# Four graph attention layers on one core: layer 3's neighbour terms by a plain transfer, masked maxima on VectorE, a changed scheduler and shared small tiles

## The chip, the cores and the metric

The kernel runs on one core of a Trainium2 chip. TensorE (PE) multiplies matrices and transposes, VectorE (DVE), ScalarE (ACT) and GpSimd (POOL) work on tiles of 128 partitions, SyncE (SP) issues DMA transfers, and so can POOL, whose transfers can add to what lies at their destination. The metric is the device time of one execution in microseconds; less is better. All data are float32, but for the int32 adjacency matrices.

## The reference, cut to what matters

There are 128 graphs of 128 nodes with 512 features (`x`), and one adjacency matrix each (`adj`). Four attention layers follow each other, each on a normalised copy of x, with a residual sum:

```python
h = jnp.maximum(_layernorm(x, axis=-1), 0.0)
x = x + _L0_gnn_ref(h, adj, W, a1, a2)              # one head, elu
h = jnp.maximum(_layernorm(x, axis=-1), 0.0)
x = x + _L1_gnn_ref(adj, h, ...)                    # 4 heads of 256, elu, then 1 head of 512
h = jnp.maximum(_layernorm(x, axis=-1), 0.0)
x = x + _L2_gnn_ref(h, adj, w_src, w_dst, b)        # one head on h itself
h = jnp.maximum(_layernorm(x, axis=-1), 0.0)
x = x + _L3_gnn_ref(h, adj, W_proj, W_att, b_att)   # 8 heads of 64
```

Layer 3, which the change is about:

```python
xh = (x @ W_proj).reshape(B, N, H, k).transpose(0, 2, 1, 3)
a_src = jnp.einsum('bhnk,hk->bhn', xh, W_att[:, :k])
a_dst = jnp.einsum('bhnk,hk->bhn', xh, W_att[:, k:])
scores = leaky_relu(a_src[:, :, :, None] + a_dst[:, :, None, :] + b_att[None, :, None, None], 0.2)
att = softmax(where((A > 0)[:, None], scores, -1e30), axis=-1)
out = relu(einsum('bhij,bhjk->bhik', att, xh))
```

## The kernel before

One graph is one generator, `graph(b)`: masks from the adjacency matrix, then `layer0`, `layer1`, `layer2`, `layer3`, then the store of x. Each `yield` hands one step (an instruction, or a `Group` of some that stay together) to the scheduler, or asks for a tile, a fork or a join. `FLYING` = 11 graphs are in the works at a time. The `Scheduler` runs while the program is built: with a hand-made table of durations (`Step.estimate`) it keeps a time at which each engine is free and each tile is written (`start`), and `issue` always emits the step that could start first, ties going to the lower `rank` (the graph's number and how far along it is). So the whole order of every engine is fixed at build time, and on the chip each engine runs its own list in order. Every instruction is emitted by one line, L256, so the profile has nearly everything on that line, and groups are told apart by tiles and shapes. Tiles of a tag come from a fixed number of buffers; `give_back` frees one.

Each layer begins with `norm_relu`: bn_stats and bn_aggr on DVE, + eps and the power -1/2 on POOL (tile `st`), nmr = -mean * rstd on DVE, then the relu with scale and bias on ACT into `h`. Layers 1 and 3 transpose `h` by four PE transposes into a PSUM bank, which ACT copies to `ht`, and project it (`projected`, weights `w1x`, `wpx`; layer 1's second part uses `w2x`). The scores of one-headed layers, and of layer 1, are masked and their maxima taken by `tensor_tensor_reduce` on DVE (in the profile CUSTOM_DVE_ANT_0, each with a DVE_READ_ACCUMULATOR2 behind it): add the mask, keep the maximum. In layers 0 and 2, dot products of h with a vector go the same way (`products<-h,u`).

Layer 3 holds a tile `sd` with 16 squares of 128 x 128: `d` (8 heads, rows are the nodes that receive, for the maxima) and `e` (8 heads, the other way round, for the matmuls). ACT copies the mask into d and its transpose into e, eight times each. The small matrix `f` (own and neighbour terms of 8 heads) is written to DRAM as 16 rows, and one accumulating DMA on POOL's queue (L612), broadcast to all partitions, adds them to d and e at once (1 MB). DVE reduces d to the maxima `mx`, adds the own term, ACT applies the leaky relu, DVE negates it. A second accumulating DMA (512 KB) adds the negated maxima to e after its eight Prelus; ACT takes the exponential, and PE multiplies e with `fx` head by head (128 x 65, the last column giving the sum). The last `LATE` = 5 graphs do without DRAM: `add_rows` makes the rows with PE transposes in PSUM and DVE adds them (six times 128 x 512 a graph).

Of the kernel before, what the change touches and what calls it, by code (L numbers as in the profile page):

```python
# [9 lines left out]
F32 = mybir.dt.float32  # L10
# [11 lines left out]
FLYING = 11  # L22
AHEAD = 1
# [19 lines left out]
class Step:  # L43
# [4 lines left out]
    def __init__(self, engine, method, args, kw):  # L48
# [7 lines left out]
        ins = [a for a in ins if isinstance(a, bass.AP)]  # L56
        self.writes = [a.tensor.name for a in outs]
# [3 lines left out]
    def estimate(self, name, outs, ins, kw):  # L61

        if name == "dma_start":
            moved = size(outs[0]) * outs[0].shape[0] * 4
            if self.engine == "POOL":
                self.moves = moved / 165e3
                return 1.0, 3
            run = 4 * min(a.shape[-1] for a in outs + ins)
            self.moves = moved / (280e3 if run > 512 else 220e3)
            return (0.5 if max(len(a.shape) for a in outs + ins) > 2 else 0.35), 1.5  # L70
# [68 lines left out]

class Scheduler:  # L140
    def __init__(self):
# [3 lines left out]
        self.moved = 0.0  # L145
# [86 lines left out]
    def start(self, step):  # L232
        t = self.engine_free.get(step.engine, 0.0)
        for r in step.reads:
            t = max(t, self.written.get(r, 0.0))
# [3 lines left out]
        return t  # L239

    def issue(self):
# [5 lines left out]
        if not ready:  # L247
            assert not self.streams, [vars(s.next) for s in self.streams]
            return False
        t, _, _, _, s = min(  # L250
            (self.start(s.next), self.rank(s), s.age, i, s) for i, s in enumerate(ready)
        )
        step = s.next
# [4 lines left out]
        end = t + step.busy + step.delay  # L258
        if step.moves:

            self.moved = max(end, self.moved) + step.moves
            end = self.moved + 0.3
        for name in step.writes:
            self.written[name] = end
        for name in step.reads + step.writes:
            self.last_use[name] = max(end, self.last_use.get(name, 0.0))
# [17 lines left out]
def kernel(  # L284
# [40 lines left out]
    small = ctx.enter_context(tc.tile_pool(name="small", bufs=FLYING + 2))  # L325
# [16 lines left out]

    def column(tag, n=1):
        return small.tile([P, n], F32, tag=tag, name=tag)
# [44 lines left out]
    def setup():  # L389
# [6 lines left out]
        w0 = yield tile_of("sd", 3, 2 * H3, P)  # L396
        w0 = w0.rearrange("p s q -> p (s q)").rearrange("p (c f) -> p c f", c=KC)
        for c in range(KC):
            yield S.dma_start(out=w0[:, c], in_=l0_w[c * P : (c + 1) * P])
# [25 lines left out]
        wa = yield tile_of("sd", 3, 2 * H3, P)  # L425
        wa = wa.rearrange("p s q -> p (s q)")[:, : H3 * 2 * K3]
# [5 lines left out]
    def fold_u(w0):  # L432
        us = [(yield bank()), (yield bank())]
        for c in range(KC):
            for i, u in enumerate(us):
# [3 lines left out]
                    rhs=w0[:, c, :],  # L439
# [6 lines left out]
        give_back(w0)  # L446
# [39 lines left out]
    def fold_w3(wa):  # L486
        pairs = wa.rearrange("p (h k) -> p h k", h=H3)
        for w in wpx:
            for s in range(2):
                prod = yield tile_of("t3", 2, D)  # L490
# [11 lines left out]
    def norm_relu(xt):  # L502
# [9 lines left out]
        yield V.scalar_tensor_tensor(nmr, mean, -1.0, rstd, ALU.mult, ALU.mult)  # L512
# [73 lines left out]

    def add_rows(cols, to):

        for g in range(0, cols.shape[1], 4):
            pt = yield bank()  # L590
            yield Group(
                [
                    T.transpose(
                        pt[:, j * P : (j + 1) * P],
                        cols[:, g + j : g + j + 1].to_broadcast([P, P]),
                        ident,
                    )
                    for j in range(4)
                ]
            )  # L600
# [4 lines left out]
    def added(cols, to, late, rows=None):  # L605

        if late:
            yield from add_rows(cols, to)
            return
        if rows is None:  # L610
            rows = yield from rows_in_dram(repeated(cols), cols.shape[1])
        yield G.dma_start(out=to, in_=rows, accum_op=ALU.add)  # L612

    def attention(own, rows, e, mask, exact=False):
# [4 lines left out]
        mx = column(f"mx{nh}", nh)  # L619
# [18 lines left out]
        neg = column(f"neg{nh}", nh)  # L638
        yield V.scalar_tensor_tensor(neg, mx, -1.0, own, ALU.mult, ALU.subtract)
        nm = column(f"nm{nh}", nh)  # L640
        yield V.scalar_tensor_tensor(nm, neg, SLOPE, neg, ALU.mult, ALU.min)
        z = column(f"z{nh}", nh)
# [20 lines left out]
        rz = column(f"rz{nh}", nh)  # L663
        yield V.reciprocal(rz, z)
        return rz

    def attended(own, other, mask, values, exact=False):
# [4 lines left out]
        rz = yield from attention(own, [pb[:, :P]], [e], mask, exact)  # L672
# [5 lines left out]
        return pa, rz  # L678
# [39 lines left out]
    def layer0(xt, mask):  # L718
        h = yield from norm_relu(xt)
        yield Until("u")  # L720
        f = column("f0", 2)
        yield from dot(h, u1, f[:, 0:1])
        yield from dot(h, u2, f[:, 1:2])
        t = yield tile_of("t0", 2, D)
        pa, rz = yield from attended(f[:, 0:1], f[:, 1:2], mask, h, exact=True)
        give_back(h)

        yield A.activation(out=t, in_=pa, func=AF.Exp, scale=rz)
        yield A.activation(out=pa, in_=pa, func=AF.Relu, scale=rz)
        yield V.scalar_tensor_tensor(t, t, 1.0, pa, ALU.min, ALU.add)  # L730
# [4 lines left out]
    def layer1(xt, mask, late):  # L735
# [22 lines left out]
        rz = yield from attention(fx[:, H1:E1], heads, heads, mask)  # L758
        for j in range(H1):
            yield A.activation(out=heads[j], in_=heads[j], func=AF.Copy, scale=rz[:, j : j + 1])  # L760
        if late:
# [7 lines left out]
        for g in range(0, FC, 4):  # L769
# [23 lines left out]
            t = yield tile_of("t1", 2, 4 * P)  # L793
# [11 lines left out]
        pa, rz = yield from attended(gx[:, 1:2], gx[:, 0:1], mask, gx[:, E2:])  # L805
        give_back(gx)
        yield V.scalar_tensor_tensor(xt, pa, rz, xt, ALU.mult, ALU.add)
        give_back(pa)

    def layer2(xt, mask):  # L810
        h = yield from norm_relu(xt)
        f = column("f0", 2)
        yield from dot(h, w_src, f[:, 0:1])
        yield from dot(h, w_dst, f[:, 1:2])
        fb = column("fb")
        yield G.tensor_tensor(fb, f[:, 0:1], b_l2, ALU.add)
        pa, rz = yield from attended(fb, f[:, 1:2], mask, h)
        give_back(h)
        yield V.scalar_tensor_tensor(xt, pa, rz, xt, ALU.mult, ALU.add)
        give_back(pa)  # L820

    def layer3(xt, mask, mask_t, late):
# [10 lines left out]
        sd = yield tile_of("sd", 3, 2 * H3, P)  # L833
        d, e = sd[:, :H3], sd[:, H3:]
        for to, m in (d, mask), (e, mask_t):
            yield A.copy(to, m.unsqueeze(1).to_broadcast([P, H3, P]))
            give_back(m)
# [9 lines left out]
        f = small.tile([P, 2, H3], F32, tag="f3", name="f3")  # L847
        yield G.tensor_tensor(f, fx[:, :, :E3].rearrange("p h s -> p s h"), b_l3, ALU.add)
        fork = yield Fork(
            added(f.rearrange("p s h -> p (s h)"), sd.rearrange("p s q -> p (s q)"), late)  # L850
# [161 lines left out]
```

## Time and profile before

| what | value |
|---|---|
| time, median of 3 runs | 3317.16 us (3317.16 to 3318.29) |
| the profiled execution's own time | 3315.37 us |
| its span | 3313.6 us |
| granted TensorE clock, mean | 0.992 |
| accumulating transfers (queue q0) | 193.48 MB, 31.2% of 16 engines' span |
| transfers issued by SP (queue q1) | 183.57 MB, 19.4% |

The profile is one execution on the chip. A row of a group reads: line, engine, operation, written tile <- read tiles, shapes, count, then busy us in all, mean ns of one, and the idle time of that engine just before the group with what ended it. The chain of waits is followed back from the last instruction, at each step to what released it. A row of windows gives the busy time of each engine in that stretch. Matmuls are pipelined and their ends modelled, so PE's busy share says that it always had something in hand, and the interval from start to start is the time that a matmul really costs.

### The profile page before, as it was taken

The numbers are of one execution on the slowest core, as the hardware profiler recorded it, in microseconds if no ns is written. First come the engines' busy times: TensorE is split into PE (matmuls) and PEld (weight loads), VectorE is DVE, ScalarE is ACT, GpSimd is POOL, SyncE is SP. The second block draws the span as 40 slices with busy tenths as digits, with TensorE's granted clock in tenths as the row PEclk, the third lists the DMA queues.
The fourth block names the chain that finished last, engine by engine and source line by source line (L and its number), as shares of the span: only waits on it lengthen the run. The fifth ranks groups of instructions, "written<-read, shape, count | busy, mean of one in ns | idle before, by whom it ended". The sixth has DMA issues, their size and how long they took to land.

```text
span 3313.6 us, 57764 instructions
## 1 busy us (share of the span) xinstructions
PE 3278.1 (99%) x16252; PEld 2577.0 (78%) x16252; DVE 2657.6 (80%) x9921; ACT 2600.8 (78%) x7060; POOL 954.6 (29%) x1791
## 2 busy tenths in 40 slices
PE   8999999999999999999999999999999999999997
PEld 5777777777777777777777777777777777777786
DVE  7778878878888888888888888788788878878866
ACT  5687887887888788788778878878887887887875
POOL 1123323332232332233233233323323323332221
PEclk8999999999999999999999999999999999999998
DMA  5155555455555545655555554555555555455441
GB/s 169 41 114 124 115 116 126 113 117 126 120 113 118 129 113 115 132 109 117 123 123 116 116 127 112 118 130 114 113 121 126 115 116 128 109 117 128 95 92 31
DMA packets 236001, 380.75 MB, mean 115 GB/s; under 512 B 57120, under 2 KB 136480, under 8 KB 219936
## 3 DMA queue, kind: packets, MB, share of 16 engines
q0 software_dynamic: 35424, 193.48, 31.2%
q1 hardware_dynamic: 196080, 183.57, 19.4%
q8 instruction: 129, 2.11, 0.3%
q14 instruction: 192, 1.57, 0.2%
q10 hardware_dynamic: 4176, 0.02, 0.1%
HBM read 309.35 MB, written 67.57 MB: 114 GB/s over the span
## 4 chain that ended last, share of the span: by engine, by line
PE 97%; DVE 2%; ACT 1%; issue 0%; POOL 0%; DMA 0%; POOLq 0%; ACTq 0%; DVEq 0%
PE bank L256 97%; DVE products L256 0%; DVE sd L256 0%; DVE t L256 0%; DVE st L256 0%; ACT sd L256 0%; DVE e L256 0%; DVE xt L256 0%; ACT ht L256 0%; POOL st L256 0%; DVE wpx L256 0%; DMA a<-in_L_gnn_a_dram 0%; DVE mx L256 0%; ACT h L256 0%; DVE m L256 0%
## 5 line engine op out<-in xcount | busy, mean ns | idle before, releaser
L256 PE MATMUL bank<-w2x,y 128*128 128x257 f32 x4096 | 971.8, 380 | 0.0
L256 PE MATMUL bank<-w1x,ht 128*128 128x344 f32 x3072 | 952.3, 453 | 0.0
L256 PEld LDWEIGHTS bank<-w2x,y 128*128 128x128 f32 x4096 | 740.2, 190 | 86.7 <-issue 2.6
L256 PEld LDWEIGHTS bank<-w1x,ht 128*128 128x128 f32 x3072 | 574.5, 191 | 245.9 <-issue 1.9
L256 POOL TENSOR_SCALAR st<-st 128x1 f32<-128x1 f32 x512 | 193.5, 378 | 1754.9 <-DVE st L256 1525.3
L256 PE MATMUL bank<-wpx,ht 128*128 128x264 f32 x2048 | 502.2, 389 | 1.4 <-ACT ht L256 1.4
L256 PEld LDWEIGHTS bank<-wpx,ht 128*128 128x128 f32 x2048 | 391.5, 192 | 119.2 <-issue 57.9
L256 ACT ACTIVATE h<-xt,st 128x512 f32<-128x512 f32 x512 | 415.8, 812 | 19.8 <-DVE st L256 18.2
L256 ACT COPY xl<-bank 128x344 f32<-128x344 f32 x384 | 170.9, 445 | 300.3 <-PE bank L256 300.2
L256 ACT ACTIVATE sd<-sd,f 128x128 f32<-128x128 f32 x1024 | 375.4, 393 | 0.0
L256 ACT ACTIVATE e<-e,nm 128x128 f32<-128x128 f32 x896 | 355.4, 399 | 6.8 <-DVE e L256 2.4
L256 DVE BATCH_NORM_STATS2 st<-xt 128x6 f32<-128x512 f32 x512 | 352.2, 688 | 0.0
L256 POOL TENSOR_TENSOR st<-st,minus_half 128x1 f32<-128x1 f32 x512 | 338.4, 661 | 42.4
L256 POOL DMA_DIRECT2D sd<-d x246 | 233.8, 951 | 192.8 <-DMA d<-r 161.0
L256 PEld LDWEIGHTS bank<-x,sd 128*128 128x128 f32 x2048 | 259.9, 193 | 17.4 <-ACT sd L256 8.1
L256 PE MATMUL bank<-et,xl 128*128 128x128 f32 x2048 | 272.1, 276 | 0.6 <-DMA et<-turned 0.6
L256 PEld LDWEIGHTS bank<-et,xl 128*128 128x128 f32 x2048 | 261.0, 193 | 11.7 <-issue 1.9
L256 PE MATMUL bank<-x,sd 128*128 128x65 f32 x2048 | 258.1, 269 | 7.1 <-ACT sd L256 7.1
L256 DVE SCALAR_TENSOR_TENSOR xt<-bank,rz,xt 128x512 f32<-128x512 f32 x256 | 191.5, 748 | 90.2 <-PE bank L256 90.1
L256 PE MATMUL bank<-h,et 128*128 128x512 f32 x512 | 245.6, 598 | 2.1 <-ACT et L256 2.1
L256 DVE STREAM_TRANSPOSE e<-e 128x512 f32<-128x512 f32 x123 | 87.5, 711 | 153.0 <-ACT e L256 152.8
L256 ACT ACTIVATE e<-e,rz 128x128 f32<-128x128 f32 x512 | 188.4, 393 | 20.9 <-DVE nm L256 18.8
(93 smaller groups left out, 5500.2 us busy)
## 6 DMA issues: line engine op xcount, KB each, us to landing
sd<-d POOLq DMA_DIRECT2D x123, 1024.0 KB, 10.3
sd<-d POOLq DMA_DIRECT2D x123, 512.0 KB, 5.1
xt<-in_x_dram SPq DMA_DIRECT2D x128, 256.0 KB
e<-d SPq DMA_DIRECT2D x128, 256.0 KB
out_dram<-xt SPq DMA_DIRECT2D x128, 256.0 KB
turned<-e SPq DMA_DIRECT2D x492, 64.0 KB
et<-turned SPq DMA_DIRECT2D x123, 256.0 KB
at<-in_adj_dram SPq DMA_DIRECT2D x32, 256.0 KB
```

Source lines behind the costliest of these rows:

```text
L256: method(*args, **kw)
```

## The change

Five things change together.

1. Layer 3 holds only `e` (tag `e3`, 8 squares). The neighbour terms for the maxima come by a plain DMA of 512 KB on SP's queue into `d3` (2 buffers), and the accumulating DMA carries only e's 8 rows. DVE adds the mask and takes the maximum in one step a head (two groups of four `tensor_tensor_reduce`) where ACT copied the mask and DVE reduced. In the last five graphs these read the rows from PSUM (`spread`). Adding the own term and negating move from DVE to POOL.
2. In `norm_relu`, nmr moves from DVE to POOL.
3. The many small tiles of 13 buffers each become shared ones with fewer: `c1`, `c4` and `f0` with 8, `f3` with 4 (it now holds f, mx and rz). `t0`, `t1` and `t3` (2 each) become one tag `t` with 5. The set-up's weights use `e3` tiles.
4. The scheduler's model: a DMA waits for the eighth one before it on its queue (`LANES`), transfers share one line ordered by when they reach it (`Transfer`), SP's delay is 2.2 or 0.6 us by size, and an accumulating DMA reads its destination.
5. The scheduler's choice: it first finds the step that can start first, and on DVE and ACT it then takes, among that engine's steps that can start within `PATIENCE` = 0.3 us of it, the one with the lowest rank.

The number of matmuls and transposes stays the same. The core of the diff, with layers 0 to 2's shared tiles and the set-up left out where they repeat it:

```diff
@@ -20,6 +20,8 @@
 FLYING = 11
+PATIENCE = .3
+LANES = 8
 AHEAD = 1
@@ -54,6 +56,8 @@
         ins = [a for a in ins if isinstance(a, bass.AP)]
+        if "accum_op" in named:
+            ins += outs
         self.writes = [a.tensor.name for a in outs]
@@ -67,7 +71,8 @@
             self.moves = moved / (280e3 if run > 512 else 220e3)
-            return (0.5 if max(len(a.shape) for a in outs + ins) > 2 else 0.35), 1.5
+            busy = 0.5 if max(len(a.shape) for a in outs + ins) > 2 else 0.35
+            return busy, (2.2 if moved > 16384 else 0.6)
         n = max(size(a) for a in outs[:1] + ins)
@@ -137,12 +142,22 @@
         self.over = False
+class Transfer:
+    through = end = 0.0
+    def __init__(self, by="", reaches=0.0, moves=0.0, writes=(), names=()):
+        self.by, self.reaches, self.moves = by, reaches, moves
+        self.writes, self.names = writes, names
 class Scheduler:
...
         self.written = {}
-        self.moved = 0.0
+        self.transfers = []
+        self.lanes = {"SP": [Transfer()] * LANES, "POOL": [Transfer()] * LANES}
         self.returned = {}
@@ -231,12 +246,35 @@
         t = self.engine_free.get(step.engine, 0.0)
+        if step.moves:
+            t = max(t, self.lanes[step.engine][len(step.calls) - 1].end)
         for r in step.reads:
...
         return t
+    def note(self, end, writes, names):
+        for name in writes:
+            self.written[name] = end
+        for name in names:
+            self.last_use[name] = max(end, self.last_use.get(name, 0.0))
+    def transfer(self, new, n, t):
+        queue = [x for x in self.transfers if x.end > t - 20]
+        i = len(queue)
+        while i and queue[i - 1].reaches > new.reaches:
+            i -= 1
+        queue.insert(i, new)
+        through = queue[i - 1].through if i else 0.0
+        for x in queue[i:]:
+            x.through = through = max(x.reaches, through) + x.moves
+            x.end = through + 0.3
+            self.note(x.end, x.writes, x.names)
+        self.transfers = queue
+        self.lanes[new.by] = self.lanes[new.by][n:] + [new] * n
     def issue(self):
@@ -247,23 +285,27 @@
             return False
-        t, _, _, _, s = min(
-            (self.start(s.next), self.rank(s), s.age, i, s) for i, s in enumerate(ready)
+        _, _, i = min((self.start(s.next), self.rank(s), i) for i, s in enumerate(ready))
+        engine, soon = ready[i].next.engine, self.start(ready[i].next)
+        if engine in ("DVE", "ACT"):
+            soon += PATIENCE
+        _, _, i = min(
+            (self.rank(s), s.age, i)
+            for i, s in enumerate(ready)
+            if s.next.engine == engine and self.start(s.next) <= soon
         )
+        s, t = ready[i], self.start(ready[i].next)
         step = s.next
...
         end = t + step.busy + step.delay
+        names = step.reads + step.writes
         if step.moves:
-            self.moved = max(end, self.moved) + step.moves
-            end = self.moved + 0.3
-        for name in step.writes:
-            self.written[name] = end
-        for name in step.reads + step.writes:
-            self.last_use[name] = max(end, self.last_use.get(name, 0.0))
+            self.transfer(Transfer(step.engine, end, step.moves, step.writes, names), len(step.calls), t)
+        else:
+            self.note(end, step.writes, names)
         s.next = None
...
@@ -487,7 +528,7 @@
-                prod = yield tile_of("t3", 2, D)
+                prod = yield tile_of("t", 5, D)
...
@@ -509,7 +550,7 @@
         yield G.tensor_tensor(out=rstd, in0=ve, in1=minus_half, op=ALU.pow)
-        yield V.scalar_tensor_tensor(nmr, mean, -1.0, rstd, ALU.mult, ALU.mult)
+        yield G.tensor_scalar(nmr, mean, rstd, -1.0, ALU.mult, ALU.mult)
         h = yield tile_of("h", 4, D)
@@ -584,31 +625,29 @@
+    def spread(cols):
+        pt = yield bank()
+        yield Group(
+            [
+                T.transpose(
+                    pt[:, j * P : (j + 1) * P], cols[:, j : j + 1].to_broadcast([P, P]), ident
+                )
+                for j in range(4)
+            ]
+        )
+        return pt
...
-            pt = yield bank()
-            yield Group(
-                [
-                    T.transpose(
-                        pt[:, j * P : (j + 1) * P],
-                        cols[:, g + j : g + j + 1].to_broadcast([P, P]),
-                        ident,
-                    )
-                    for j in range(4)
-                ]
-            )
+            pt = yield from spread(cols[:, g : g + 4])
...
-    def added(cols, to, late, rows=None):
-        if late:
-            yield from add_rows(cols, to)
-            return
-        if rows is None:
-            rows = yield from rows_in_dram(repeated(cols), cols.shape[1])
+    def added(to, rows):
@@ -616,7 +655,8 @@
-        mx = column(f"mx{nh}", nh)
+        c = yield tile_of(f"c{nh}", 8, 5 * nh)
+        mx, neg, nm, z, rz = (c[:, i * nh : (i + 1) * nh] for i in range(5))
...
@@ -718,15 +754,16 @@
-        f = column("f0", 2)
+        f = yield tile_of("f0", 8, 3)
...
-        t = yield tile_of("t0", 2, D)
...
@@ -830,11 +868,9 @@
-        sd = yield tile_of("sd", 3, 2 * H3, P)
-        d, e = sd[:, :H3], sd[:, H3:]
-        for to, m in (d, mask), (e, mask_t):
-            yield A.copy(to, m.unsqueeze(1).to_broadcast([P, H3, P]))
-            give_back(m)
+        e = yield tile_of("e3", 3, H3, P)
+        yield A.copy(e, mask_t.unsqueeze(1).to_broadcast([P, H3, P]))
+        give_back(mask_t)
@@ -844,18 +880,47 @@
-        f = small.tile([P, 2, H3], F32, tag="f3", name="f3")
+        f = yield tile_of("f3", 4, 4, H3)
+        f, mx, rz = f[:, :2], f[:, 2], f[:, 3]
...
-        fork = yield Fork(
-            added(f.rearrange("p s h -> p (s h)"), sd.rearrange("p s q -> p (s q)"), late)
-        )
+        if late:
+            fork = yield Fork(add_rows(f[:, 1], e.rearrange("p h q -> p (h q)")))
+        else:
+            rows = yield from rows_in_dram(repeated(f.rearrange("p s h -> p (s h)")), 2 * H3)
+            d = yield tile_of("d3", 2, H3, P)
+            yield S.dma_start(out=d.rearrange("p h q -> p (h q)"), in_=rows[:, : H3 * P])
+            fork = yield Fork(added(e.rearrange("p h q -> p (h q)"), rows[:, H3 * P :]))
+        for g in range(0, H3, 4):
+            if late:
+                d = yield from spread(f[:, 0, g : g + 4])
+                part = d.rearrange("p (h q) -> p h q", h=4)
+            else:
+                part = d[:, g : g + 4]
+            yield Group(
+                [
+                    V.tensor_tensor_reduce(
+                        out=part[:, j],
+                        in0=part[:, j],
+                        in1=mask,
+                        scale=1.0,
+                        scalar=LOWEST,
+                        op0=ALU.add,
+                        op1=ALU.max,
+                        accum_out=mx[:, g + j : g + j + 1],
+                    )
+                    for j in range(4)
+                ]
+            )
+            if late:
+                give_back(d)
+        give_back(mask)
+        if not late:
+            give_back(d)
...
-        mx = column("mx3", H3)
-        yield V.tensor_reduce(mx, d, AX.X, ALU.max)
-        yield V.tensor_tensor(mx, mx, f[:, 1], ALU.add)
+        yield G.tensor_tensor(mx, mx, f[:, 1], ALU.add)
...
-        yield V.tensor_scalar(mx, mx, -1.0, None, ALU.mult)
+        yield G.tensor_scalar(mx, mx, -1.0, None, ALU.mult)
@@ -865,13 +930,11 @@
-        rows = (yield Join(fork)) if fork else None
-        fork = yield Fork(added(mx, e.rearrange("p h q -> p (h q)"), late, rows))
+        ef = e.rearrange("p h q -> p (h q)")
+        fork = yield Fork(add_rows(mx, ef) if late else added(ef, (yield Join(fork))))
...
-        ef = e.rearrange("p h q -> p (h q)")
...
-        t = yield tile_of("t3", 2, D)
-        rz = column("rz3", H3)
+        t = yield tile_of("t", 5, D)
```

## The prediction

> **What bounds the kernel now.** First the page, for the busy shares and the chain's shares:
>
> ```profile
> PE 3278.1 (99%) x16252; PEld 2577.0 (78%) x16252; DVE 2657.6 (80%) x9921; ACT 2600.8 (78%) x7060; POOL 954.6 (29%) x1791
> PE 97%; DVE 2%; ACT 1%; issue 0%; POOL 0%; DMA 0%; POOLq 0%; ACTq 0%; DVEq 0%
> ```
>
> PE is idle for 3313.6 - 3278.1 = 35.5 us of the whole span. The chain of waits, in order of time, says where:
>
> ```profile
> 46.05 0.68 DVE products L256
> ...
> 72.21 0.88 DVE e L256 x2
> ...
> 82.75 3128.28 PE bank L256 x15535
> ...
> 3263.89 1.88 DVE sd L256 x3
> ...
> 3300.11 1.12 DVE mx L256
> ```
>
> From 82.75 to 3211 us the chain is one unbroken run of PE. No other engine ends a wait there. The windows (us; then length, busy time and count of PE, PEld, DVE, ACT, POOL; PE clock, DMA share, GB/s) give sizes:
>
> ```profile
> 0.00:100.00 100.00, 83.92 (x321) 57.45 (x322) 73.74 (x273) 55.16 (x143) 15.88 (x41) 0.85 0.49 148
> 1600.00:1700.00 100.00, 100.00 (x497) 78.66 (x497) 81.51 (x306) 80.49 (x220) 31.14 (x58) 1.00 0.54 121
> 3252.00:3314.00 62.00, 43.34 (x245) 35.75 (x244) 37.04 (x99) 30.00 (x71) 4.53 (x14) 0.83 0.07 26
> ```
>
> The first 100 us hold 16.1 us of the idle time, the last 62 hold 18.7; the middle has none, at clock 1.00. A graph costs 126 matmul records at 4.97 to 4.99 per us, 25.2 us, and its PE instructions are the same before and after. In the steady part every form keeps its own interval between starts whatever stands beside it (217 ns for 257 columns, 289 for 344, 429 for 512). Adding these up for all that ran before 90 us, 34.8 us were lost by then (idle time and lower clock); the tail from 3235 us loses another 24.6. So the change can win in two places only, start and tail, and can lose anywhere.
>
> **The change, part by part.** The rows it touches (busy us in all, then mean ns):
>
> ```profile
> L256 DVE TENSOR_REDUCE mx<-sd 128x8 f32<-128x1024 f32 x128 | 155.4, 1214 | 1.1 <-DMA sd<-d 1.0
> L256 DVE CUSTOM_DVE_ANT_0 e<-e,m 128x128 f32<-128x128 f32 x512 | 117.7, 286 | 0.3 <-issue 0.3
> L256 DVE SCALAR_TENSOR_TENSOR st<-st 128x1 f32<-128x1 f32 x512 | 80.5, 157 | 32.9 <-POOL st L256 32.6
> L256 ACT COPY sd<-m 128x1024 f32<-128x1024 f32 x128 | 134.8, 1053 | 0.0
> L256 POOL TENSOR_SCALAR st<-st 128x1 f32<-128x1 f32 x512 | 193.5, 378 | 1754.9 <-DVE st L256 1525.3
> sd<-d POOLq DMA_DIRECT2D x123, 1024.0 KB, 10.3
> ```
>
> Layer 3's mask copy: ACT loses 1.05 us a graph. The maximum: DVE loses the 1.21 us reduction and two small operations of 0.16 us, and gains eight masked maxima; a group of four in layer 1 (the second row) takes 0.92 us from first start to last end, so eight take 1.8 us. Nmr, four a graph, leaves DVE: 4 x 0.16 = 0.63 us. DVE: -1.21 - 0.32 + 1.8 - 0.63 = -0.3 us a graph. Both engines have idle time in the steady part (18.5 and 19.5 us in 100), PE none: this is worth nothing there. What hides it is PE's own stream. Without that cover it would be worth at most 0.3 us of DVE and 1.05 us of ACT a graph.
>
> The transfers: the accumulating one halves, from 1 MB to 512 KB (10.3 to 5.1 us to landing, by the other accumulating transfer's row), and stays two issues a graph on POOL's queue. SP's queue gets one more issue a graph (0.34 us by e<-d's issue), of 512 KB. No row gives its landing: between 1.7 us (512 KB at the 311 GB/s of the 20 to 40 us window) and 10.3 us (both halves sharing one rate); I take 5.1, since the halves start together, from the same rows. It is behind e<-d, turned and et<-turned on SP. The masked maxima stand in DVE's order about where the reduction stood, so up to some 10 us the new transfer is not later than the old one. From layer 3's exponential to its matmuls, the built order leaves 4 to 5 us where 0.2 to 0.6 were left before. I cost the transfer at nothing (DVE's spare time hides about 1 us of lateness in a graph); above that, PE waits.
>
> Nmr and two layer-3 operations on POOL: six small operations a graph. Alone, one takes 0.22 us; the mean is 0.378. POOL's timeline shows what makes the difference:
>
> ```profile
> 1606.49 0.22 POOL L256 TENSOR_SCALAR st<-st 128x1 f32<-128x1 f32 x1 [5.75 <-DVE st L256]
> 1615.08 0.93 POOL L256 TENSOR_SCALAR st<-st 128x1 f32<-128x1 f32 x1 [5.13 <-DVE st L256]
> ```
>
> The second ran from 1615.08 to 1616.01 beside DVE's xt<-t,xt and t<-y (1614.90 to 1615.91). So an operation costs 0.22 to 0.93 us, and 6 x 0.378 = 2.3 us a graph, which POOL (29% busy) has. What counts is the path through it. From the end of layer 2 to the transposes of h, PE has 12.75 us of other work in the order before, 7.5 us from end to start in the one after (8.4 from start to start; added up from row intervals). On this path, for every second graph: DVE's add into xt, bn_stats, bn_aggr (done at 3.7 us after the start of layer 2's last matmul), POOL's +eps and pow of two graphs, then layer 3's f, behind which nmr of both graphs queues, and ACT: relu of the graph before, one Prelu, layer 0's exponential (waits for PE until 6.8), relu. Unheld: nmr at 5.5 and 5.9, relu ends 8.25 of 8.4: no wait, with 0.15 us to spare. Held for one group of four masked maxima, which DVE issues just after bn_aggr (0.9 us): 9.2, a wait of 0.8 us. For the other graphs 1.7 us is spare. So the steady part costs between 0 and 0.8 us per two graphs. In the trace of before no POOL operation overlaps such a group at all, so it does not show whether the group holds POOL to its end or lets it in between two of its members. I take 0: by the nearest row, a masked maximum alone is 0.286 us, a hold of the size of the spare time.
>
> The Trainium skill, SBUF — State Buffer, section on SBUF's two separate sides, says that VectorE with two SBUF inputs and GpSimd share one port pair as an exclusive lock, the loser being fully blocked for the instruction. The 0.93 us row agrees. It speaks against moving work to POOL beside new two-input operations; a lock per instruction would cost at most 0.29 us at a time, an estimated 0.1 us per two graphs (0.1 x 64 pairs = 6 us), and the whole group 0.8.
>
> The scheduler and the shared tiles: no new instruction; they change order and buffers. Four f3 buffers are enough: by PE's work in the built order a graph is in layer 3 for 59 us, 2.3 graphs at 25.2 us each; c1, c4 and f0 live shorter still with eight. At nothing, then; without that reserve a graph would wait for the release, a PE wait. At the start PE waited for DVE, which was full from 44 to 82 us. In the built order the largest excess of DVE work ahead of a PE step over PE's own work falls from 18.4 to 9.9 us, so at most 8.5 us is won. But DVE's order has it wait at its head for graph 0's xl with 18.9 us of work done, where it had 24.5: 5.6 back, 2.9 left. I take 4.7, somewhat below the middle; -1 to +9 for the range. In the tail the last graph's path from its second layer-1 projection took 61.2 us. Its operations shrink by nothing much (six adds 3.7, reduction 1.1, against four adds 2.45, eight maxima 1.8 and POOL's hops 0.5); but 16.6 us of that path was queueing behind others, and DVE's whole work after this point falls from 39.1 to 34.3 us. Between 0 and 4.8; I take 3, as DVE ends most of these waits.
>
> Sum, against the profiled execution: its own 3315.4 (span 3313.6 and 1.8 around it) - 4.7 - 3 + 0 = 3307.7. The median of the runs shown, 3317.2, is 1.8 above it, so 3309.5.
>
> **The rivals.** (a) Start and tail shrink, the stream holds: 3309.5, own range 3303 (9 + 5 won) to 3313. For it: the unbroken PE run. (b) Nothing visible: the head-of-line waits eat the start, the tail's end is set by PE's own steps, or small waits in the stream (0.1 us x 64 = 6) take back what is won: 3313 to 3322, about 3317. For it: the same PE work, and idle time that is only 1% of the span. (c) Slower: nmr on POOL becomes what PE waits for, at the transposes of h of every second graph. Price: 0.3 to 0.8 us x 64 = 19 to 51 us, less the 7.7: 3329 to 3360, most likely 3332 (0.35). It decides from the point where that relu ends more than 8.4 us after the start of layer 2's last matmul, thus with any hold above 0.15 us. For it: the 0.93 row and 5 us of reserve given up. Against: a PE wait shifts the whole stream, and the holds need not meet every pair. (d) The steady order is different but the ends are as before, because the adds of the last five graphs still set them: it falls within (b).
>
> **How the numbers follow.** Chances: (a) 0.46, (b) with (d) 0.25, (c) 0.29. A measurement of this kernel can't tell less than 0.2%, 6.6 us, from no change: faster is below 3310.5, slower above 3323.8. (a) wins 7.7, up to 14 and hardly under 4, so I put 0.36 of its 0.46 below 3310.5; 0.04 of (b) goes there too (one end wins, the stream loses nothing) and 0.03 of it above 3323.8, with all of (c). Faster 0.40, same 0.28, slower 0.32. The predicted time is (a)'s, 3309.5. The range goes from 3301 to 3334, which leaves the upper half of (c) out.
>
> **What would show it.** Right: PE 100.00 busy and x497 to 499 in every 100 us of the middle; PE's waits in all under 35 us; POOL's st operations near 0.38 us; the first 100 us with 87 us or more of PE. The mechanism of (c) would show as a wait of PE on ACT's h every 50 us and a pace below 4.97 records per us. A wait of DVE on the d3 transfer, or of PE on layer 3's f or e in the middle, would make the costing of the transfers wrong.

## The result and the profile after

The changed kernel took 3331.32 us (median of 5 runs, 3330.23 to 3333.2) against 3317.52 us before (5 runs): 13.8 us slower, ratio 1.0042, 95% interval 1.0027 to 1.0057. The profiled execution is the one of 3333.2 us, with a span of 3331.4 us, 17.8 us above the span of before. That execution is 1.9 us above its own median, and the profiled one of before (3315.37 us) 2.2 below its median, so 4 of the 17.8 us are scatter between executions. Differences of 2 or 3 us in what follows may be no more than that.

The page of the changed kernel, the busy shares:

```profile
PE 3286.5 (99%) x16252; PEld 2577.7 (77%) x16252; DVE 2752.8 (83%) x11063; ACT 2478.1 (74%) x6932; POOL 1208.4 (36%) x2559
```

PE has the same 16252 records. Its windows (columns as before: length, then busy us and count of PE, PEld, DVE, ACT, POOL; PE clock, DMA share, GB/s):

```profile
0.00:100.00 100.00, 77.93 (x274) 51.32 (x275) 62.88 (x211) 47.80 (x126) 14.41 (x42) 0.81 0.47 140
1600.00:1700.00 100.00, 100.00 (x499) 78.73 (x498) 84.54 (x344) 76.58 (x216) 38.20 (x79) 1.00 0.50 121
3269.00:3331.00 62.00, 44.30 (x263) 36.73 (x262) 41.98 (x148) 29.24 (x71) 10.20 (x33) 0.89 0.07 26
```

The middle is as full as before. In the first 100 us PE did 274 records where it had done 321, and it was DVE that did less there too: 62.88 us against 73.74.

For sizes I use the sum that the forecast used: every PE instruction that has started, at the interval its form keeps at full clock. What the elapsed time is above that sum is called lost. All the PE work adds up to 3244.7 us, in every kernel below. The loss splits in three: the start (until 100 us of PE work are done), the steady part (until 3000 us are done) and the tail.

| lost, us | start | steady | tail | sum |
|---|---|---|---|---|
| before | 34.9 | 4.2 | 29.7 | 68.8 |
| changed | 45.1 | 5.5 | 36.0 | 86.6 |

So 10.2 us went at the start, 6.3 in the tail and 1.3 in between: 17.8, the difference of the spans.

**The start.** By the two windows of the first 100 us PE was idle 6.0 us longer (busy 77.93 against 83.92), and its granted clock was 0.81 against 0.85, which is worth an estimated 4 us of PE work. Most of the added idle time is waits for h, the normalised x that PE transposes: three in the changed kernel, 6.1 us together, and two before, 0.9 us.

```profile
54.05 0.81 PE L301 MATMUL bank<-ident,h 128*128 128x128 f32 x4 [2.15 <-ACT h L301]
67.46 0.65 PE L301 MATMUL bank<-ident,h 128*128 128x128 f32 x4 [1.69 <-ACT h L301]
85.98 0.66 PE L301 MATMUL bank<-ident,h 128*128 128x128 f32 x4 [2.30 <-ACT h L301]
```

```profile
71.47 1.12 PE L256 MATMUL bank<-ident,h 128*128 128x128 f32 x4 [0.59 <-ACT h L256]
82.75 1.11 PE L256 MATMUL bank<-ident,h 128*128 128x128 f32 x4 [0.31 <-ACT h L256]
```

DVE stood still longer as well. The waits of DVE between 12 and 95 us (us in all, times, longest), in the changed kernel and then in the kernel before:

```profile
DVE products L301 <- ACT h L301: 6.0, 2, 3.5
DVE r L301 <- ACT xl L301: 4.0, 2, 3.4
DVE e L301 <- PE bank L301: 3.3, 4, 1.4
DVE t L301 <- ACT bank L301: 3.2, 3, 1.8
```

```profile
DVE e L256 <- PE bank L256: 2.9, 2, 1.5
DVE m L256 <- PE bank L256: 2.9, 2, 2.4
DVE t L256 <- ACT bank L256: 2.0, 2, 1.7
DVE st L256 <- POOL st L256: 1.7, 4, 0.7
```

All lines of that answer add up to 23.7 us in the changed kernel and 13.2 before. One of these waits, 3.46 us for h at 24.61 us, can be followed on ACT. The timeline of ACT in the changed kernel (start, duration, instruction, idle time before it):

```profile
23.29 0.59 ACT L301 COPY ht<-bank 128x512 f32<-128x512 f32 x1 [2.80 <-PE bank L301]
23.77 0.81 ACT L301 ACTIVATE h<-xt,st 128x512 f32<-128x512 f32 x1
```

and in the kernel before:

```profile
19.83 1.67 ACT L256 ACTIVATE h<-xt,st 128x512 f32<-128x512 f32 x2
22.53 0.59 ACT L256 COPY ht<-bank 128x512 f32<-128x512 f32 x1 [1.03 <-PE bank L256]
```

Before, two relus h ran at 19.8 us, ahead of a copy that waited for PE. In the changed order the copy stands ahead; ACT waits 2.80 us for PE, the relu starts at 23.77, h is done at 24.58, and DVE stands still until then. Both lists were fixed at build time.

**The tail.** The last graph's path, from its first transpose (graph 127, layer 0) to the end, took 179.8 us before and 180.5 after. The PE work still to be done at that first transpose was 150.2 us before and 144.6 after. The tail loses the difference: 180.5 - 144.6 = 35.9 against 179.8 - 150.2 = 29.6.

### The profile page after: what moved, and what is told of

Same layout as the page of the kernel before. It is cut to its first block, busy times and chain, and to the rows that moved or that the text cites. A ratio compares the mean times of both kernels' runs of the same rounds, so it can differ in the third digit from the quotient of the medians.

```text
span 3331.4 us, 59808 instructions
## 1 busy us (share of the span) xinstructions
PE 3286.5 (99%) x16252; PEld 2577.7 (77%) x16252; DVE 2752.8 (83%) x11063; ACT 2478.1 (74%) x6932; POOL 1208.4 (36%) x2559
## 5 line engine op out<-in xcount | busy, mean ns | idle before, releaser
L301 POOL TENSOR_SCALAR st<-st 128x1 f32<-128x1 f32 x1024 | 351.4, 347 | 661.8 <-DVE st L301 539.5
L301 ACT ACTIVATE e<-e,c 128x128 f32<-128x128 f32 x1408 | 532.7, 400 | 77.8 <-DVE e L301 59.0
L301 ACT ACTIVATE e<-e,f 128x128 f32<-128x128 f32 x1152 | 386.1, 392 | 2.6 <-POOL st L301 1.5
L301 POOL DMA_DIRECT2D e<-d x246 | 233.3, 948 | 389.1 <-DMA d<-r 208.7
L301 PEld LDWEIGHTS bank<-x,e 128*128 128x128 f32 x2048 | 269.4, 193 | 91.4 <-issue 56.7
L301 POOL TENSOR_TENSOR st<-st,minus_half 128x1 f32<-128x1 f32 x512 | 298.5, 585 | 29.4
L301 PE MATMUL bank<-x,e 128*128 128x65 f32 x2048 | 259.0, 270 | 8.9 <-ACT e L301 8.9
L301 DVE TENSOR_TENSOR y<-bank,b 128x512 f32<-128x512 f32 x256 | 176.1, 688 | 97.3 <-PE bank L301 95.8
L301 DVE CUSTOM_DVE_ANT_0 d<-d,m 128x128 f32<-128x128 f32 x984 | 225.3, 284 | 34.9 <-DMA d<-d 33.8
L301 POOL TENSOR_SCALAR m<-m 128x128 f32<-128x128 f32 x128 | 143.3, 1119 | 288.9 <-DVE m L301 266.1
```

Of the source, the lines that this page charges most:

```text
L301: method(*args, **kw)
```

## The experiments

Start, steady part and tail are those of one profiled execution; the times are medians against the kernel before on the same chip in the same set.

| run | start | steady | tail | time, us | ratio, 95% interval |
|---|---|---|---|---|---|
| changed | 45.1 | 5.5 | 36.0 | 3331.3 | 1.0027 to 1.0057 |
| e1 old scheduler | 44.9 | 141.6 | 33.6 | 3468.0 | 1.0443 to 1.0478 |
| e2 before, new scheduler | 40.0 | 104.6 | 38.6 | 3430.4 | 1.0329 to 1.036 |
| e3 patience 0 | 47.6 | 45.2 | 30.9 | 3370.3 | 1.0149 to 1.0179 |
| e4 nmr on DVE | 47.9 | 4.7 | 31.4 | 3330.2 | 1.0027 to 1.0057 |
| e5 own tiles | 43.8 | 5.6 | 35.8 | 3332.1 | 1.0027 to 1.006 |
| e6 old layer 3 | 40.6 | 37.7 | 32.6 | 3353.9 | 1.0088 to 1.0129 |
| e7 before, nmr on POOL | 37.8 | 8.8 | 30.8 | 3325.5 | 1.0012 to 1.0033 |
| e8 old transfer model | 37.2 | 18.4 | 34.8 | 3337.0 | 1.0045 to 1.0075 |
| e9 no patience in the tail | 45.3 | 5.5 | 35.9 | 3332.5 | 1.0025 to 1.0055 |
| e10 no lanes | 42.5 | 7.2 | 34.4 | 3333.2 | 1.0027 to 1.0057 |
| e11 one delay | 39.8 | 14.2 | 33.1 | 3336.4 | 1.0034 to 1.0066 |
| e12 e8's model early, e9 | 38.1 | 5.7 | 36.8 | 3327.4 | 1.0018 to 1.0037 |
| e13 slow PE early | 39.5 | 5.5 | 34.8 | 3326.4 | 1.0015 to 1.0039 |
| e14 e13 and e8's model early | 38.5 | 6.3 | 34.5 | 3326.1 | 1.0018 to 1.004 |
| e15 e8's model early, e4 | 40.0 | 4.8 | 31.9 | 3320.6 | 1.0000 to 1.0022 |
| e16 patience 0.4 | 34.8 | 7.3 | 32.9 | 3321.3 | 0.9998 to 1.0021 |
| e17 patience 0.5 | 44.6 | 5.9 | 32.2 | 3328.5 | 1.002 to 1.0043 |
| e18 patience 0.4, e4 | 33.1 | 4.9 | 34.7 | 3325.2 | 1.0014 to 1.0034 |

### Which half carries it: the scheduler or the kernel's steps (e1, e2, e3, e4)

The theory was that the new scheduler's order carries the loss; the rivals were nmr on POOL and layer 3's new steps.

e1: the whole `Scheduler`, `Step` and `Group` of before in the changed kernel.

```diff
-        _, _, i = min((self.start(s.next), self.rank(s), i) for i, s in enumerate(ready))
...
+        t, _, _, _, s = min(
+            (self.start(s.next), self.rank(s), s.age, i, s) for i, s in enumerate(ready)
+        )
...
-            self.transfer(Transfer(step.engine, end, step.moves, step.writes, names), len(step.calls), t)
+            self.moved = max(end, self.moved) + step.moves
```

> The changed kernel with the scheduler of before (its durations, its one line of transfers, its choice); layer 3, nmr on POOL and shared tiles stay. Theory A, the new scheduler's order at start and tail carries the loss: 3314 to 3321 us, loss by 100 us near 35 (44.9 in the changed kernel), after 3200 us near 29 (35.4). Rival B, nmr on POOL: 3328 or more, the start loses 43 or more. Rival C, layer 3's new steps: 3325 to 3333, the tail still loses 34 or more.

e2: the same the other way round, the new scheduler in the kernel before.

```diff
-        t, _, _, _, s = min(
-            (self.start(s.next), self.rank(s), s.age, i, s) for i, s in enumerate(ready)
-        )
+        _, _, i = min((self.start(s.next), self.rank(s), i) for i, s in enumerate(ready))
...
-            self.moved = max(end, self.moved) + step.moves
+            self.transfer(Transfer(step.engine, end, step.moves, step.writes, names), len(step.calls), t)
```

> The kernel before with the whole new scheduler, nothing else. Theory A: 3327 to 3334 us, start loss 42 or more. Rivals B and C: 3314 to 3320, start loss near 35.

e3:

```diff
-PATIENCE = .3
+PATIENCE = 0.0
```

> The changed kernel with a patience of 0, so DVE and ACT take the step that can start first again. Theory A1, the patience: at most 3321 us and a start loss of at most 38. Theory A2, the model of the transfers: 3328 or more, the start loss stays above 43. Rivals B and C: as A2.

e4:

```diff
-        yield G.tensor_scalar(nmr, mean, rstd, -1.0, ALU.mult, ALU.mult)
+        yield V.scalar_tensor_tensor(nmr, mean, -1.0, rstd, ALU.mult, ALU.mult)
```

> The changed kernel with nmr back on DVE. Rival B: at most 3321 us, the start loss at most 38. Theory A: 3328 to 3335, start loss 42 to 47.

Every one of the first three came out worse than both kernels, by up to 152 us against the kernel before. By the letter e1 fits rival B (3328 or more, start 43 or more) and e3 fits A2 (3328 or more, start above 43), but no theory had foreseen where the time went. The steady part, which neither the kernel before nor the changed one loses time in, stalls when the two halves are mixed. The largest row of PE's waits between 150 and 3190 us, first e1's, then e2's, then the changed kernel's, which is its only one:

```profile
PE bank L258 <- ACT et L258: 63.3, 112, 3.2
```

```profile
PE bank L301 <- POOL st L301: 58.9, 57, 2.3
```

```profile
PE bank L301 <- ACT et L301: 0.4, 1, 0.4
```

112 waits in e1, 57 in e2, one in the changed kernel. They are about half of what the steady part lost (63.3 of 141.6 us and 58.9 of 104.6); the rest was not followed up. Thus the kernel's new steps and the new scheduler belong together: with both, the stream holds; with one of them, it doesn't. Which of the steps e1 stalls on, layer 3's or the shared tiles, was not run under the old scheduler. Theory A (the scheduler alone) fell, as e1 has the late start (44.9) without it, and C (layer 3 alone) fell, as e1 is far from its 3325 to 3333. e4 took the rival of nmr down: the same ratio as the changed kernel (1.0042), with a worse start and a better tail.

### What of the kernel's steps is left (e5, e6, e7), and the model of the transfers (e8)

e5:

```diff
-        c = yield tile_of(f"c{nh}", 8, 5 * nh)
+        c = yield tile_of(f"c{nh}", 13, 5 * nh)
...
-        t = yield tile_of("t", 5, D)
+        t = yield tile_of("t0", 2, D)
```

(and so for f0, f3, t1 and t3)

> The changed kernel with the tiles unshared: 13 buffers for c1, c4, f0 and f3, and t0, t1, t3 with 2 each again. If the shared tiles make the start late: start loss at most 38, time at most 3324 us. Rival, the order at the start follows small differences of modelled costs and not the tiles: start loss stays at 42 to 50, time 3326 to 3336.

e6 puts layer 3 and the set-up's use of its tiles back (`sd`, two mask copies, one accumulating transfer of 1 MB, `tensor_reduce`):

```diff
-        e = yield tile_of("e3", 3, H3, P)
+        sd = yield tile_of("sd", 3, 2 * H3, P)
...
+        yield V.tensor_reduce(mx, d, AX.X, ALU.max)
```

> The changed kernel with layer 3 and the set-up's weight tiles as before; new scheduler, nmr on POOL, shared tiles stay. If layer 3's steps carry the start and tail: start loss at most 40, and the steady part stalls no more than in the changed kernel. If the new scheduler was fitted to the new layer 3: losses in the steady part of 50 us or more, as with the kernel before under the new scheduler (3430 us).

e7, in the kernel before:

```diff
-        yield V.scalar_tensor_tensor(nmr, mean, -1.0, rstd, ALU.mult, ALU.mult)
+        yield G.tensor_scalar(nmr, mean, rstd, -1.0, ALU.mult, ALU.mult)
```

> The kernel before with nmr on POOL, nothing else. If POOL's hold by DVE's two-input operations matters (the forecast's rival): a steady loss above 20 us with PE waiting for ACT's h. If only the modelled order changes: start loss moves by up to 10 us either way, steady waits come with other operands than h.

e8:

```diff
-            self.transfer(Transfer(step.engine, end, step.moves, step.writes, names), len(step.calls), t)
+            self.moved = max(end, self.moved) + step.moves
+            end = self.moved + 0.3
```

(with the delay of 1.5, no lanes, no read of the destination)

> The changed kernel with the transfer model of before (one line, delays 1.5, no lanes, no read of the destination), patience .3 kept. If the model of transfers makes the start late: start loss at most 40 and a steady part with stalls at waits for transfers (over 20 us). If it is patience: start loss 43 or more, graph 3's first DVE step still after 50 us, tail 34 or more.

The shared tiles make no difference that can be told here: e5's start is within 1.3 us and its tail within 0.2 us of the changed kernel's, and DVE's order differs in some 150 of 7461 steps. e6 loses 37.7 us in the steady part, less than the 50 that were expected, and has a start of 40.6 in one execution, the slower of two that are 7.4 us apart; the 4.5 us that this start is better are less than a small change of order moves it (e16 below). e2, which has nmr and the tiles of before as well, lost 104.6 in the steady part, so these too bear on whether the stream holds. e7 costs 7.4 us in the kernel before (3325.47 against 3318.07); its profiled execution loses 2.9 us more at the start and 4.6 in the steady part. In the changed kernel the same move in the other direction (e4) made the start 2.8 worse. One edit, either way, and no better start. e8 gains 7.9 us at the start and loses 12.9 in the steady part: with this kernel the new model of the transfers keeps the stream fed better than the old one, and the order it gives has the later start.

### The tail, and the parts of the transfer model (e9, e10, e11, e12)

e9:

```diff
+LAST = 121
...
-        if engine in ("DVE", "ACT"):
+        if engine in ("DVE", "ACT") and min(s.age for s in self.streams) < LAST:
             soon += PATIENCE
```

> The changed kernel with the patience off once graph 121 is the oldest in the works. If patience holds back the last graph in the tail: everything before 3000 us as in the changed kernel (loss 50 to 51), the tail loses 29 to 31 where it lost 35, time 3325 to 3328 us. Rival, the tail's 35 is this order's luck: tail 33 to 37, time 3329 to 3333.

e10:

```diff
-LANES = 8
+LANES = 64
```

> The changed kernel with 64 transfers in flight in the model where it had eight. If the count of eight makes the start late: start loss at most 40. If the delays by size do: start loss 43 or more, graph 0's first matmul of layer 1's attention after 88 us.

e11:

```diff
-            return busy, (2.2 if moved > 16384 else 0.6)
+            return busy, 1.5
```

> The changed kernel with one delay of 1.5 us for all of SP's transfers in the model (2.2 and 0.6 by size in the change); eight in flight and the order by arrival stay. If the delays make the start late: start loss at most 40. If the lanes do: 43 or more.

e12 has e9's edit, and this one, which uses the model of before while the scheduler's own time is below 100 us:

```diff
+WARM = 100
...
-        if step.moves:
+        if step.moves and t < WARM:
+            reaches = t + step.busy + (3 if step.engine == "POOL" else 1.5)
+            self.moved = max(reaches, self.moved) + step.moves
...
+        elif step.moves:
```

> The changed kernel with the transfer model of before for the first 100 us of the scheduler's own time, and the patience off in the tail. If the causes are these two and the steady order settles whatever the start was: start loss 36 to 39, no more than 7 lost from there to 3100 us, tail 29 to 31, time 3316 to 3322 us. Rival, the steady order depends on how the start leaves the graphs: the steady part stalls by 10 us or more, time above 3325.

The patience in the tail fell at once (35.9 against 36.0). The start is 39.8 with one delay (e11) and 42.5 without lanes (e10); read as shares of the model's price the delays would be the larger one, but e16 below moves the start by more than either with no change of the model, so these shares are not shown. e12 shows that a better start and a full steady part can be had together: start 38.1, steady 5.7. Its tail did not get shorter, as e9 had already said, and so it misses its 3316 to 3322 by 5 us.

What e1 to e12 say of the tail: the PE work left at the last graph's first transpose is 149.3 to 150.2 us in the four kernels with the old layer 3 (before, e2, e6, e7) and about 144.6 us in each one with the new, whatever the scheduler, the patience or the tiles. So these 5 us or so of the tail belong to layer 3. The path itself goes from 175.5 us (e3) to 181.2 (e12) with the new layer 3.

### A slow PE, or a draw of the order (e13 to e18)

e13 (the granted clock was 0.50 to 0.58 from 20 to 45 us):

```diff
+COLD = 45
...
-        self.engine_free[step.engine] = t + step.busy
-        end = t + step.busy + step.delay
+        busy = step.busy * (2 if step.engine == "PE" and t < COLD else 1)
+        self.engine_free[step.engine] = t + busy
+        end = t + busy + step.delay
```

> The changed kernel, with the scheduler's durations of PE doubled for the first 45 us of its own time (the granted clock was 0.50 to 0.58 from 20 to 45 us there). If DVE and ACT wait at the start because their order was planned with a PE at full clock: their waits for PE and for each other get shorter, start loss at most 41 (44.9). If the delay of transfers in the model alone sets the start: 43 to 47.

e14 is e13 with the early part of e12.

```diff
+        busy = step.busy * (2 if step.engine == "PE" and t < COLD else 1)
...
+        if step.moves and t < WARM:
```

> As the run before, with the transfer model of before for the first 100 us too. If the two causes add up: start loss 31 to 35 (37.0 with the transfer model alone), steady loss at most 8, tail 35 to 37, time 3320 to 3325. If the start is a draw of the order: anywhere from 35 to 45.

e15 is the early part of e12 with e4's edit.

```diff
+        yield V.scalar_tensor_tensor(nmr, mean, -1.0, rstd, ALU.mult, ALU.mult)
...
+        if step.moves and t < WARM:
```

> The changed kernel with the transfer model of before for the first 100 us and nmr on DVE. If nmr on POOL makes the last graph's path long (180.5 us against 175.9 with nmr on DVE alone): tail 30 to 32, start 37 to 40, time 3316 to 3321. If that was the order's draw: tail 33 to 37.

e16:

```diff
-PATIENCE = .3
+PATIENCE = .4
```

> The changed kernel with a patience of 0.4 in place of 0.3: the same work on every engine, another order. If start and tail have one cause each in the change: start loss 43 to 47 and tail 34 to 37, as in the changed kernel. If they are draws of an order that hangs on small differences: start or tail moves by more than 3 us, and the steady part may stall by 10 us or more.

e17:

```diff
-PATIENCE = .3
+PATIENCE = .5
```

> The changed kernel with a patience of 0.5. With 0.3 the start lost 44.9, with 0.4 34.7. If a longer patience is what helps the start: start loss at most 36. If it is a draw of the order: anywhere from 35 to 48, the steady part within 4 to 15 us, the work left behind the last graph's first transpose stays 144.6 us.

e18 is e16 with e4's edit.

```diff
-PATIENCE = .3
+PATIENCE = .4
...
+        yield V.scalar_tensor_tensor(nmr, mean, -1.0, rstd, ALU.mult, ALU.mult)
```

> The changed kernel with a patience of 0.4 and nmr on DVE: the best start seen with the new layer 3 and the place of nmr that had the short tail (31 to 32). If these two add up: start 34 to 37, tail 31 to 32, time 3313 to 3319 us, level with the kernel before. If the order is a draw: start above 38 or tail above 33, time 3320 or more.

e13's start is 5.6 us better (39.5), as was expected if the order was planned for a PE at full clock. With the old transfer model beside it (e14) it is 38.5, no better than with that model alone (38.1): the gains do not add up, and the 31 to 35 expected was wrong. e16 to e18 show why single gains of this size say little. With the same instructions on every engine, a patience of 0.3, 0.4 and 0.5 us loses 45.1, 34.8 and 44.6 us at the start. The windows of e16:

```profile
0.00:100.00 100.00, 82.42 (x323) 56.48 (x324) 69.92 (x233) 51.56 (x136) 15.93 (x45) 0.86 0.51 148
1600.00:1700.00 100.00, 100.00 (x500) 78.83 (x499) 84.50 (x343) 77.09 (x217) 37.77 (x80) 1.00 0.51 120
```

323 records in the first 100 us, as many as before (321), and a full middle. e16's profiled execution (3321.56 us) is a typical one of its eight (median 3321.3). Of its 10.3 us, PE's busy time accounts for 4.5 (82.42 against 77.93) and the granted clock, 0.86 against 0.81, for an estimated 5. 0.1 us in a rule for near ties is thus worth 10 us at the start, and this is as much as the whole loss there. So the start is a draw of the built order: parts of the change move it, but no part was shown to own it. The draws are not centred on the kernel before: of the changed kernel and the eighteen others only e16 (34.8) and e18 (33.1) start no later than its 34.9. Whether that is its luck or something that the change took away is open. e15 and e4 have the short tails (31.9 and 31.4), yet e18, which has nmr on DVE as well, has 34.7: the last graph's path is drawn too, on top of layer 3's fixed share.

e18's profiled execution was the fastest of its nine (3319.2 us, where the median is 3325.2, range 3319.2 to 3329.62). Its start of 33.1 us is therefore a good one and not a typical one. No kernel tried beat the one before; e15 and e16 come to about 0.1% of it, intervals 1.0000 to 1.0022 and 0.9998 to 1.0021.

## Why the prediction was wrong, step by step

**The steady stream: right, for the reasons given.** PE 100.00 busy, x498 to 502 in each window read from 200 to 3100 us, one wait of 0.4 us. That ACT would lose 1.05 us a graph: 80.49 to 76.58 busy in the 100 us window, at 3.97 graphs, 0.98 us. For DVE the forecast said -0.3 us a graph, and that was wrong: the busy time rose by 3.0 us in the window, 0.76 a graph. The masked maxima cost what was used, 0.92 us for a group of four from start to last end. One term that was mis-sized is nmr: busy time counts overlapping operations once, and of the 80.5 us of its row only 20.7 are covered by no other operation of DVE in the trace of before, 0.16 us a graph where 0.63 was taken off. It cost nothing, as DVE had the idle time. POOL: 2.3 us a graph forecast, 7.1 us in the window, 1.8 a graph.

**The transfers at nothing: right.** DVE did wait for the new one, as the row of the masked maxima says (busy, mean, then idle time before them):

```profile
L301 DVE CUSTOM_DVE_ANT_0 d<-d,m 128x128 f32<-128x128 f32 x984 | 225.3, 284 | 34.9 <-DMA d<-d 33.8
...
e<-d POOLq DMA_DIRECT2D x246, 512.0 KB, 7.1
```

44 waits of at most 2 us, 33.8 us in all, hidden in DVE's idle time; PE never waited for layer 3 in the middle. The accumulating 512 KB lands in 7.1 us (median), where 5.1 was taken.

**Rival (c), nmr on POOL: its time came, its mechanism did not.** It was priced at 3332 us, and 3331.3 was measured; that is a coincidence, and the measured time lies inside the stated range only because (c) had widened it. (c) was to cost 0.3 to 0.8 us for every second graph, and in the steady part no such wait exists. The waits for h at the start are not its work either: with nmr on DVE (e4) the start is no better. The question left open, whether a group of four masked maxima holds POOL to its end, has an answer in the timeline of the changed kernel, POOL first and DVE below:

```profile
1446.39 0.49 POOL L301 TENSOR_SCALAR st<-st 128x1 f32<-128x1 f32 x2 [0.36 <-DVE st L301]
```

```profile
1446.35 0.26 DVE L301 CUSTOM_DVE_ANT_0 e<-e,m 128x128 f32<-128x128 f32 x1
...
1446.53 0.29 DVE L301 CUSTOM_DVE_ANT_0 e<-e,m 128x128 f32<-128x128 f32 x1
...
1446.74 0.28 DVE L301 CUSTOM_DVE_ANT_0 e<-e,m 128x128 f32<-128x128 f32 x1
...
1446.96 0.28 DVE L301 CUSTOM_DVE_ANT_0 e<-e,m 128x128 f32<-128x128 f32 x1
```

Two POOL operations ran from 1446.39 to 1446.88, inside the group. Of some 210 such POOL operations on `st` that overlap a group, all but three took at most 0.38 us, where one alone takes 0.22, and the longest 0.53: the group does not hold POOL to its end. The Trainium skill (SBUF — State Buffer, on SBUF's two separate sides) has the lock last for one instruction. These rows agree: 0.38 is 0.16 more than 0.22, less than the 0.21 us from one member's start to the next. Taking 0 here was right.

**The start: wrong, and this is the step.** "In the built order the largest excess of DVE work ahead of a PE step over PE's own work falls from 18.4 to 9.9 us, so at most 8.5 us is won ... I take 4.7". It lost 10.2. The working counted the work that stands ahead of each PE step and only one of DVE's waits (graph 0's xl), and it read PE's waits as waits for DVE: in the trace of before PE waits 16.1 us in the first 130 us, of which DVE's results end 0.7 us and ACT's 10.2 (DVE can stand behind some of these). The new order brought 23.7 us of waits of DVE against 13.2, and 6.1 us of waits of PE for ACT's h against 0.9. A count of work ahead is a bound for an engine that never waits; at the start DVE and ACT wait for PE, at about half clock from 20 to 45 us, and PE for them. The lower clock, an estimated 4 us more, stood in no term of the gain. Two of the forecast's own signs say the same: 87 us or more of PE in the first 100 became 77.93, and PE's waits, to be under 35 us, add up to 40. That the patience and the model change the start by 6 to 10 us is shown (e8, e13, e16); that every microsecond of DVE's waits is one of the start's is not: e8 has nearly as much idle DVE in its first 95 us as the changed kernel (30.8 against 34.6 us with the first wait for the adjacency matrices) and a start of 37.2.

**The tail: wrong in this step.** "Between 0 and 4.8; I take 3, as DVE ends most of these waits." It looked at the last 61 us of the path, from behind layer 1's second projection, and at DVE's work beside it. That stretch did get 3.2 us shorter (61.2 to 58.0 us), as was taken; but the path from the last graph's first transpose did not (179.8 to 180.5), since the part ahead of the stretch grew by 3.9 us, and the PE work that could hide the path fell by 5.6 us, which was nowhere in the sum. That this goes with layer 3 is shown over all runs; why the new layer 3 leaves less work behind (graphs ahead of the last are further on by then) was only read from the order, where a graph of the middle has about 5 us less PE work between its first and its last PE step.

**The ranges** of -1 to +9 and 0 to 4.8 for the two ends share this fault: both ends were taken as terms that a change of order can hardly make worse. Over all the kernels here the lost time goes from 33 to 48 us at the start and from 30 to 39 in the tail.

## What to carry to other kernels

Where every engine's order is fixed at build time by a model, a change of the work and the model that orders it are one thing: parts of this change cost 36 to 152 us where they left the other half as it was (e1, e2, e3, e6), the whole of it 14. When the main stream is full, look at the start and the tail as draws: try two or three neighbouring values of a tie rule before reading a gain or loss of a few tenths of a per cent as the work of an edit. And price a tail as the last item's path less the work left to hide it, both of them, not by the operations on the path alone.

## What the runs showed of the hardware

TensorE's granted clock was 0.50 to 0.58 from 20 to 45 us of the changed kernel although PE was busy 17.34 of the 20 us from 20 to 40. The Trainium skill (TensorE: Matmul & The Clock Gate, Part 1) says the clock falls to half after an idle window of some 3.4 us; this stretch has no such idle time, its waits are 0.3 to 0.73 us each; but about half of its matmuls, 48 of the 86 records from 20 to 45 us, have two columns only. Whether the gaps or the narrow matmuls keep the clock down was not tried. In the kernel before, the clock was at 0.50 from 20 to 35 us and at 0.84 from 35 to 40, so the slow stretch was shorter there.
